# Cross attention on one core: a turn for every operation of the scheduler in place of a rank for each task

## The chip, the core and the metric

The kernel runs on one core of one Trainium2 chip. The metric is the time of one execution on the device in microseconds. A core has a matrix engine (TensorE, PE in the profile, with PEld for its weight loads), VectorE (DVE), ScalarE (ACT), GpSimd (POOL), and SyncE (SP), whose queue issues nearly all DMAs here. Each engine carries out its instructions in the order in which they stand in the program, and waits on semaphores for what the others deliver.

## The reference

`x` is (2, 2048, 640); `ctx_768` is (2, 128, 384), of which the first 124 rows are the text and the last 4 the adapter's tokens. There are 8 heads, in float32 throughout.

```python
query = hidden_states @ Wq
keyt, valt = enc @ Wk, enc @ Wv
hs = _mha(query, keyt, valt)                       # text: 2048 queries, 124 keys
ca_q1 = jnp.einsum('btc,th->bch', ca, Wq_ca)       # 384 rows, one per channel
indices = np.linspace(0, 384 - 1, unet_size).astype(np.int64)
ca_q1 = ca_q1[:, indices, :]
ca_hs1 = _mha(ca_q1, residual, residual)           # 384 different queries, 2048 keys
ca_hs2 = _mha(ca_hs1 @ Wq, ca @ Wk_ca, ca @ Wv_ca) # 4 keys
out = (hs + ca_hs2) @ Wout + b_out + residual
```

## The kernel before

**What is computed where.** The tokens of the two batches are cut into 8 blocks of 512 and 16 units of 256 (two tiles of 128 tokens each). For a block, x is loaded and transposed on VectorE (`xt`), multiplied with the adapter's folded weights (`yz_block`, tile `pyz`) and with Wq (`queries` for the first two blocks, `queries_fast` for the others, tile `pq`; the fast form computes a 2x2 split of the product with seven multiplications and sums of x and of Wq, and VectorE adds the parts up). For a unit, `text_scores` makes the scores of two tiles (`sc`), `softmax` their exponentials (`p`), which go to HBM and come back turned (`kept`, then `pT` by four loads); `hidden` multiplies them with the values (`ph`, copied to `hs`), and `text_out_fast` multiplies with Wout in four chains of products (`po`), each added by VectorE onto the rows of x. For a batch, `adapter` makes the scores of the 384 different queries twice: once for their maxima over 24 pieces (tile `s`, 4 PSUM banks, read by VectorE into `mx`), and once for their exponentials over 24 pieces (`s`, read by ScalarE into `ea`), which `contract` multiplies with the values (`acc`); `second` does the attention over four tokens and writes 384 rows (`o2`) to HBM. At the end GpSimd gathers a row of `o2` for each token onto a finished tile by an indirect DMA (`add_second`, line 2129), and SyncE stores the tile. Unit 15 has its gather ahead of its products, and is stored by half rows.

**Shapes of matmul.** A float32 matmul stands in the trace as two. Most products use four 128x32 tiles of the array side by side (`by_columns`, line 222: `pq`, `po`; line 210: `ph`, `acc`); `sc` uses two of 64x128, `s` four of 32x128, `pyz` eight of 64x32; transposes and the setup use the full 128x128.

**The order of the work.** It is fixed while the program is built. Each part above is a task: a Python generator that yields operations (`Do`) and starts further tasks (`Fork`). `Desk` replays the kernel with estimated durations: in `run` it takes, for each engine, the operations whose inputs and buffers are known, finds the earliest time at which one can start, and among those ready at that time picks the one with the lowest `order`, plus for TensorE a price for changing the tile shape (`change`). The engine with the earliest start issues. The instructions of an engine are kept in just that order. `order` is the rank of the task, or of the operation, plus an offset for the task out of the table `RANKS`, set by its name and number. An operation that may run on more than one engine stands in the queues of all of them, and the first to take it has it. Buffers are `Room`s of so many slots (`banks` for PSUM, `rows` for the tiles of x that become output, `hss` for `hs`); a slot is free from the time at which its last user is estimated to end. Durations come from `matmul`, `by_columns`, `transpose`, `__getattr__` (the other engines), `dma`, and `_mode` for a change of shape. A transfer's time is a queue of one channel: so long to issue, so long on the channel, and 2.8 us until it has landed.

In `stored`, a tile of a unit whose batch's `o2` isn't known yet when it is finished would be written to HBM and read back later (`early_`); otherwise it waits for its gather.

Of the kernel before, what the change touches and what calls it, by code (L numbers as in the profile page):

```python
# [8 lines left out]
F32 = mybir.dt.float32  # L9
# [50 lines left out]
class Task:  # L60
    def __init__(self, gen, rank, key, more):
        self.gen, self.rank, self.key, self.more, self.last = gen, rank, key, more, Event()


class Desk:
# [4 lines left out]
    WHOLE, SWITCH, LEAVE, ANOTHER = (P, P), 328.5, 9.9, 185.7  # L70
# [6 lines left out]
    MORE = {  # L77
        "v_transpose": 0.025, "v_stream_shuffle": 0.09, "v_scalar_tensor_tensor": 0.07, "v_reciprocal": 0.035,
        "a_activation": 0.045,
    }  # L80
    COLD = 5.2
    TAIL = {"PE": 0.25, "DVE": 0.18, "ACT": 0.2, "POOL": 0.25, "SP": 0.1, "NONE": 0.0}


    RANKS = {
        "adapter": {0: 1, 1: 2},
        "chain": {2: 8, 4: -11, 5: 7, 6: -2, 8: -11, 11: -4, 14: 11, 15: 16, 19: -14, 24: -4, 25: 3, 30: 3.1,
            32: 4, 34: 10, 36: 2, 41: 0.5, 42: 1, 43: 0.5, 44: -10, 45: -10, 48: -8, 50: -5, 51: -5, 52: 7,
            54: 10, 55: 10, 56: 10, 68: -4, 76: -3, 81: 2, 86: 2, 87: 3},
        "contract": {0: 5, 1: 4.5, 2: 8, 3: 8},  # L90
        "halves_away": {1: -4, 2: -2, 4: 4, 6: 6},
        "keys": {0: -10},
        "probabilities": {3: -8, 5: -4, 8: 12, 9: -3, 10: -2, 12: 6, 13: 6, 15: 7},
        "queries_fast": {0: 5, 3: 4},
        "rest_back": {1: 11, 4: 5, 7: 8, 9: 9, 10: 5, 14: 2},
        "second": {0: 2.3},
        "softmax": {0: 5, 2: -7, 3: 6.2, 4: -4, 7: -11, 8: 2, 10: -5, 12: -20, 14: -3, 17: 9, 20: -2, 21: 7,
            22: 7, 25: -5, 29: 2, 30: 6},
        "sums_of_wq": {0: 5.7},
        "text_scores": {0: -8, 1: 3.4, 12: 9},  # L100
        "values_weights": {0: -18},
        "x_load": {1: 4.2, 4: 5},
        "y_rows": {2: 2, 3: 6, 4: 4},
        "y_weights": {0: 1},
        "yz_block": {2: 16, 5: 3.5, 6: 5},
    }

    def __init__(self, tc):
        self.tc, self.nc, self.now, self.spent, self.mode = tc, tc.nc, 0.0, 0.0, None
        self.free = {e: 0.0 for e in self.ENGINES}  # L110
        self.queue = {e: [] for e in self.ENGINES}
        self.events, self.landed, self.channel, self.log, self.begun = {}, 0.0, 0.0, [], {}

# [6 lines left out]
    def begin(self, gen, rank):  # L120
        name = gen.__name__
        n = self.begun[name] = self.begun.get(name, -1) + 1
        task = Task(gen, rank, (name, n), self.RANKS.get(name, {}).get(n, 0.0))
        task.last.t = self.now
        self.go_on(task, None)

    def go_on(self, task, value):
        while True:
# [7 lines left out]
        op.task, op.at = task, Event()  # L136
# [45 lines left out]
    def issue(self, t, engine, op):  # L182
        for e in op.engines:
            self.queue[e].remove(op)
        self.now, self.spent, self.landed, self.engine = t, 0.0, None, engine
# [23 lines left out]
    def matmul(self, out, lhsT, rhs, **kw):  # L209
        self.pin(self.nc.tensor.matmul(out, lhsT, rhs, **kw))  # L210
        n = 1
        for size in rhs.shape[1:]:
            n *= size
# [3 lines left out]
        self.spent += self.slow() * (1 if one else 2) * max(n / 1.2, 107) / 1e3 / at_once  # L217

    def by_columns(self, out, lhsT, rhs, **kw):
# [3 lines left out]
        n = 1  # L223
        for size in rhs.shape[1:]:
            n *= size
        self._mode(P, P)
        self.spent += 2 * max(n / 1.2, 107) / 1e3

    def transpose(self, out, in_, ident):
        self.pin(self.nc.tensor.transpose(out, in_, ident))  # L230
        self._mode(P, P)
        self.spent += self.slow() * 0.115
# [4 lines left out]
    def __getattr__(self, name):  # L237

        side, _, what = name.partition("_")
        engine = {"v": self.nc.vector, "a": self.nc.scalar, "g": self.nc.gpsimd}[side]  # L240
        base, each = {"v": (0.06, 1.04), "a": (0.13, 0.77), "g": (0.1, 2.1)}[side]
# [2152 lines left out]
```

## Time and profile before

| what | value |
|---|---|
| median of 3 runs | 582.21 us (582.02 to 582.29) |
| the profiled execution | 581.8 us, of which 580.1 us are its span |
| granted clock of TensorE | 1.000 |
| first matmul, last matmul's end | 1.13 us, 576.4 us |
| scores `s` from and to | 52.7 us to 459 us |
| gathers from and to | 342.7 us to 567.5 us |
| DMA | 112.71 MB, 194 GB/s over the span |

The span runs from the first to the last instruction that the profiler saw on the core; times of single instructions are given from its start. A row of a group reads: line, engine, operation, what is written and what is read, shapes and count, then busy time and the mean of one in ns, then the idle time of the engine ahead of them and what ended it. A row in order of time reads: start, length, engine, line, operation, tiles, shapes, count, and in brackets the idle time ahead of it and what ended it.

### The profile page before, as it was taken

The numbers are of one execution on the slowest core, as the hardware profiler recorded it, in microseconds if no ns is written. First come the engines' busy times: TensorE is split into PE (matmuls) and PEld (weight loads), VectorE is DVE, ScalarE is ACT, GpSimd is POOL, SyncE is SP. The second block draws the span as 40 slices with busy tenths as digits, with TensorE's granted clock in tenths as the row PEclk, the third lists the DMA queues.
The fourth block names the chain that finished last, engine by engine and source line by source line (L and its number), as shares of the span: only waits on it lengthen the run. The fifth ranks groups of instructions, "written<-read, shape, count | busy, mean of one in ns | idle before, by whom it ended". The sixth has DMA issues, their size and how long they took to land.

```text
span 580.1 us, 19105 instructions
## 1 busy us (share of the span) xinstructions
PE 570.3 (98%) x8115; PEld 308.4 (53%) x8115; DVE 391.7 (68%) x645; ACT 309.8 (53%) x869; POOL 141.6 (24%) x200
## 2 busy tenths in 40 slices
PE   9999999999999999999999999999999999999997
PEld 8885334555555545455455445454455545545453
DVE  2446799999999756356999999973455253444443
ACT  2413376686566898689847447277877613002020
POOL 9102112012206411120114326050140312403241
PEclk9999999999999999999999999999999999999999
DMA  8897866979766888234999969999549487799995
GB/s 245 196 263 131 199 94 187 179 201 172 182 184 137 217 157 221 82 113 149 219 284 247 230 152 236 270 227 275 142 105 266 112 211 155 181 263 247 250 249 139
DMA packets 153039, 112.71 MB, mean 194 GB/s; under 512 B 83701, under 2 KB 126581, under 8 KB 152954
## 3 DMA queue, kind: packets, MB, share of 16 engines
q1 hardware_dynamic: 147322, 100.80, 67.5%
q0 software_dynamic: 5632, 10.69, 11.3%
q8 instruction: 64, 1.05, 0.8%
q14 instruction: 21, 0.17, 0.1%
HBM read 71.23 MB, written 40.22 MB: 192 GB/s over the span
## 4 chain that ended last, share of the span: by engine, by line
PE 64%; DVE 16%; DMA 8%; ACT 6%; issue 4%; SPq 1%; DVEq 0%; ACTq 0%
PE po L222 25%; PE pq L222 9%; PE ph L210 6%; DVE mx L245 6%; PE acc L210 5%; PE s L210 4%; PE pq L210 4%; PE sc L210 3%; ACT ea L245 3%; DMA kept<-eb 3%; DMA pT<-kept 2%; ACT p L245 2%; DVE m L245 2%; DVE q L245 2%; DVE eb L245 2%
## 5 line engine op out<-in xcount | busy, mean ns | idle before, releaser
L245 DVE TENSOR_REDUCE mx<-s 128x4 f32<-128x2048 f32 x48 | 109.4, 2280 | 4.1 <-PE s L210 4.1
L245 ACT ACTIVATE ea<-s 128x2048 f32<-128x2048 f32 x48 | 91.0, 1897 | 24.2 <-PE s L210 23.9
L245 ACT ACTIVATE p<-sc,m 128x124 f32<-128x124 f32 x256 | 90.2, 383 | 10.2 <-DVE m L245 9.7
L222 PE MATMUL po<-wout_sums,hs 128*32 128x320 f32 x1024 | 77.3, 433 | 0.0
L222 PE MATMUL po<-wout_sb,hs 128*32 128x320 f32 x960 | 74.2, 433 | 0.7 <-DVE x_more L245 0.7
L222 PE MATMUL pq<-xt,wq_sb 128*32 128x256 f32 (+1 forms) x928 | 66.3, 418 | 0.5 <-DVE mt L245 0.5
L245 DVE TENSOR_TENSOR x_more<-x_more,po 128x320 f32<-128x320 f32 x72 | 34.3, 483 | 45.5 <-PE po L222 45.4
L2129 POOL DMA_INDIRECT x_more<-o,query x18 | 27.9, 1550 | 124.3 <-DVE x_more L245 92.5
L245 ACT ACTIVATION_READ_ACCUMULATOR p<-sc,m 128x1 f32 x256 | 57.8, 226 | 0.0
L245 ACT COPY hs<-ph 128x512 f32<-128x512 f32 (+1 forms) x34 | 18.5, 551 | 65.8 <-PE ph L210 65.2
L222 PEld LDWEIGHTS po<-wout_sums,hs 128*32 128x32 f32 x1024 | 32.9, 110 | 34.1 <-issue 1.8
L210 PE MATMUL acc<-ea,y_sb 128*32 128x384 f32 (+2 forms) x768 | 51.0, 385 | 0.0
L222 PEld LDWEIGHTS po<-wout_sb,hs 128*32 128x32 f32 x960 | 30.4, 110 | 33.1 <-issue 1.5
L245 DVE TENSOR_REDUCE m<-sc 128x4 f32<-128x496 f32 x64 | 40.0, 662 | 10.4 <-PE sc L210 10.4
L245 DVE TENSOR_TENSOR last_rows<-last_rows,po 128x320 f32<-128x320 f32 x56 | 26.7, 481 | 27.9 <-PE po L222 27.5
L210 PE MATMUL ph<-pT,vpad 128*32 128x256 f32 x768 | 45.3, 380 | 0.1
L245 POOL TENSOR_TENSOR p<-p,r 128x992 f32<-128x992 f32 x8 | 14.8, 1846 | 125.0 <-DVE r L245 125.0
L222 PEld LDWEIGHTS pq<-xt,wq_sb 128*32 128x32 f32 x928 | 27.8, 109 | 29.6 <-issue 13.5
L245 DVE STREAM_TRANSPOSE eb<-p 128x1024 f32<-128x1024 f32 x32 | 39.4, 1233 | 5.6 <-DMA kept<-eb 5.5
L210 PEld LDWEIGHTS sc<-kmain,q 64*128 64x128 f32 x512 | 32.1, 187 | 13.7 <-issue 5.5
L210 PE MATMUL sc<-kmain,q 64*128 64x124 f32 x512 | 38.4, 285 | 0.2 <-ACT p L245 0.2
L245 ACT CAST rests<-landing 128x512 fp32r<-128x512 f32 x30 | 18.7, 635 | 36.2 <-PE sc L210 28.0
(216 smaller groups left out, 847.6 us busy)
## 6 DMA issues: line engine op xcount, KB each, us to landing
kept<-eb SPq DMA_DIRECT2D x32, 512.0 KB, 3.8
pT<-kept SPq DMA_DIRECT2D x64, 256.0 KB, 8.2
landing<-away SPq DMA_DIRECT2D x60, 128.0 KB, 4.3
xi<-in_x_dram SPq DMA_DIRECT2D x56, 128.0 KB, 4.6
x_more<-in_x_dram SPq DMA_DIRECT2D x18, 320.0 KB, 6.8
out_dram<-x_more SPq DMA_DIRECT2D x16, 320.0 KB, 6.6
last_rows<-in_x_dram SPq DMA_DIRECT2D x14, 320.0 KB, 7.2
out_dram<-last_rows SPq DMA_DIRECT2D x14, 320.0 KB, 10.0
```

Source lines behind the costliest of these rows:

```text
L210: self.pin(self.nc.tensor.matmul(out, lhsT, rhs, **kw))
L222: self.pin(self.nc.tensor.matmul(out[j : j + 32], lhsT[:, j : j + 32], rhs, **kw))
L245: self.pin(getattr(engine, what)(*args, **kw))
L2129: desk.pin(nc.gpsimd.indirect_dma_start(out=t, out_offset=None, in_=o2_of[b], in_offset=bass.IndirectOffsetOnAxis(ap=query[:, st : st + 1] ...
```

## The change

The table `RANKS` is emptied, and a table `TURNS` gives each of the 2353 operations of the 572 tasks a number of its own, by the task's path (the number of its start within its parent) and the operation's place in it. The first numbers of a path are: 2 the idle work, 4 the first loads, 5 to 16 the setup, 17 to 54 the blocks, 55 the adapter with 55.1 for the second batch, 56 to 71 the units 0 to 15. Where a path has turns, the price for a change of shape is 0, and TensorE may take an operation that is ready up to `AHEAD` = 0.368 us after the first. The estimates of durations are replaced as well: entering and leaving a tile shape have a price each, a matmul some ns more, VectorE and GpSimd wait for each other in operations with two inputs, a transfer has its own time to issue and on the channel, and a queue holds eight transfers in flight. What was done by counters in the code (when a slot of x, of q or of `hs` is free, when a tile is finished) are operations of their own on no engine. A finished tile of a unit below 15 always waits for its gather; the way by HBM is gone. The matmuls are the same and as many.

```diff
@@ class Desk
-    START = {(P, P): 0.107, (64, P): 0.143, (P, 64): 0.107, (64, 32): 0.1, (P, 32): 0.03}
-    DRAIN = {
-        ((P, P), (32, P)): 0.136, ((P, P), (64, P)): 0.035, ((P, P), (P, 64)): 0.056, ((P, P), (P, 32)): 0.067,
-        ((32, P), (P, 32)): 0.049, ((P, 64), (P, P)): 0.07, ((P, P), (P, P)): 0.0,
-    }
-    DRAINS = {(64, P): 0.172, (32, P): 0.108, (P, 32): 0.115}
+    AHEAD, IDLE = 0.368, 0.0
+    ENTER = {(P, P): 0.104, (64, P): 0.143, (64, 32): 0.16, (P, 32): 0.024, (32, P): 0.006}
+    EXIT = {(P, P): 0.07, (P, 32): 0.114}
+    SLOTS = 8
...
+    TURNS = {
+        ".1": [94], ".2": [8, 10, 18, 12, 20, 15, 7, 22, 0, 23, 28, 24, 19, 31, 32, 86], ".3": [60], ".4": [1, 13,
...
+        ".64.3.8": [2323], ".64.3.9": [2327, 2322, 2346], ".64.3.10": [2320, 2317, 2352], ".64.3.11": [2294, 2332,
+        2299, 2287, 2305, 2318, 2314, 2310], ".64.3.12": [2301, 2300, 2306, 2312], ".64.3.13": [2316, 2324],
+        ".64.3.14": [2303, 2304], ".65.1": [2014, 2062], ".65.2": [1122, 1214], ".65.2.1": [1135, 1130, 1132, 1138,
...
+        ".69.3.8": [1828], ".69.3.9": [1791, 2201, 2232], ".69.3.10": [1830, 2127, 2148], ".69.3.11": [1738, 1744,
...
+        ".71.3.12": [2350, 2344], ".71.3.13": [2319, 2329, 2321, 2336, 2339, 2342, 2309, 2347], ".71.3.14": [2328,
+        2311, 2341, 2345], ".71.3.15": [2335, 2338], ".71.3.16": [2334, 2333], ".72": [257, 259, 201, 282, 304, 312,
...
+    RANKS = {}
@@ begin, go_on
+        self.parent.forks += 1
+        task.path = f"{self.parent.path}.{self.parent.forks}"
...
+        op.task, op.at, op.num = task, Event(), task.ops
+        task.ops += 1
@@ change, order, run
-        if mode is None or mode == self.mode:
+        if mode is None or mode == self.mode or self.mode is None or self.TURNS:
             return 0.0
-        return self.LEAVE if self.mode == self.WHOLE else self.SWITCH if mode == self.WHOLE else self.ANOTHER
+        return self.CHANGE.get(self.KINDS[self.mode] + self.KINDS[mode], 0.0)
 
     def order(self, op):
+        if op.task.path in self.TURNS:
+            return self.TURNS[op.task.path][op.num]
         return (op.order() if callable(op.order) else op.order) + op.task.more
...
-                    t = min(x[0] for x in found)
+                    first = min(x[0] for x in found)
+                    ahead = self.AHEAD if e == "PE" else 1e-9
                     t, op = min(
-                        (x for x in found if x[0] <= t + 1e-9),
-                        key=lambda x: self.order(x[1]) + self.change(x[1].mode),
+                        (x for x in found if x[0] <= first + ahead),
+                        key=lambda x: self.order(x[1]) + self.change(x[1].mode) + self.IDLE * (x[0] - first),
                     )
@@ issue
+        if self.pairs:
+            self.spent += max(0.0, self.port[self.SHARED[engine]] - t)
+            self.port[engine] = t + self.spent
@@ _mode
+        if mode != self.mode:
+            self.spent += self.EXIT.get(self.mode, 0.0)
         if mode != self.mode or self.idle:
-            self.spent += self.START.get(mode, 0.0)
-            self.spent += self.DRAIN.get((self.mode, mode), self.DRAINS.get(self.mode, 0.1))
+            self.spent += self.ENTER.get(mode, 0.05)
@@ dma
-    def dma(self, out, in_, us, issue=0.45, more=2.8):
+    def dma(self, out, in_, us, issue=0.5, more=2.7):
 
         self.pin(self.nc.sync.dma_start(out, in_))
-        self.spent += issue
+        self.transfer("SP", us, issue, more)
+
+    def transfer(self, side, us, issue, more=2.7):
+
+        flights = self.flights[side]
+        self.spent = max(self.spent, flights.pop(0) - self.now) + issue
         self.channel = max(self.channel, self.now + self.spent) + us
         self.landed = self.channel + more
+        flights.append(self.landed)
@@ probabilities
-                lambda: dma(pT[R * j : R * (j + 1)].rearrange("p i k h a -> p i (k h a)"), by_keys[j], 1.1),
+                lambda: dma(pT[R * j : R * (j + 1)].rearrange("p i k h a -> p i (k h a)"), by_keys[j], 1.2, 0.48),
@@ add_second
-        desk.spent += 1.9
-        desk.landed = desk.now + desk.spent + 6.5
+        desk.transfer("POOL", 1.5, 1.57)
@@ one of the operations in place of a counter
+    def free_x(b, sb):
+
+        yield Do("NONE", lambda: None, [("x", b, sb)])
+        yield Do(
+            "NONE", lambda: None, [("used", b, sb, "yz"), ("used", b, sb, "q")], frees=[(xslots, xt[b, sb][1])]
+        )
@@ stored
+        yield Do("NONE", lambda: None, both)
         b, st = tiles(m)[k]
         t, i, _ = xr_of[m][k]
         rows_out = out[b, st * P : (st + 1) * P, :]
-        own = []
-        if gather_last[m] and not desk.known(("o2", b)):
-            part = hbm.tile([P, H], F32, tag=f"early_{m}_{k}", name=f"early_{b}_{st}")
-            op = yield Do("SP", lambda: dma(part, t, 1.3), both, frees=[(rows, i)])
-            yield Do("NONE", lambda: None, [op.at, ("o2", b)])
...
-            op = yield Do("SP", load, needs=[(rows, 1), (ending, 1)], rank=-1)
-            t, i, own = op.value, op.slots[0][0], [(ending, op.slots[1][0])]
-            both = [op.at]
-        if gather_last[m]:
-            op = yield Do("POOL", lambda: add_second(t, b, st), [*both, ("o2", b), "query"])
-            both = [op.at]
-        yield Do("SP", lambda: dma(rows_out, t, 1.3), both, frees=[(rows, i)] + own)
+        op = yield Do("POOL", lambda: add_second(t, b, st), [*both, ("o2", b), "query"])
+        yield Do("SP", lambda: dma(rows_out, t, 1.3, 0.41), frees=[(rows, i)])
```

More of the change, by code (lines that the diff above doesn't have):

```diff
@@ L1255, in queries @@
             own = [(qslots, 1)] if n not in q_of else []
-            op = yield Do("PE", part, [*after, "wq4"], needs=[(banks, 1), *own], mode=(P, P))
+            op = yield Do("PE", part, [*after, "wq4"], needs=[(banks, 1), *own], mode=(P, 32))
             pq, s, q = op.value, op.slots[0][0], q_of[n][0]
@@ L1879, in product @@
                     return po
-                op = yield Do("PE", product, [here, ("w2", u)], needs=[(banks, 1)])
+                op = yield Do("PE", product, [here, ("w2", u)], needs=[(banks, 1)], mode=(P, 32))
                 op = yield Do(
@@ L2243, in chain @@
                 op = yield Do(
-                    "PE", product, after + at + ready, needs=[(banks, 1)] if k == 0 else [], mode=(P, P), rank=rank
+                    "PE", product, after + at + ready, needs=[(banks, 1)] if k == 0 else [], mode=(P, 32), rank=rank
                 )
@@ L2266, in chain @@
-                ends.setdefault((m, i), []).append(op.at)
-                if not tile_left[m, i]:
-                    yield Fork(stored(m, i, ends[m, i]), 1)
+        reads = {(i, u): [] for i in range(2) for u in range(2)}
+        for n, steps in enumerate(chains):
+            for _, _, (place,) in steps:
+                reads[place].append(("sum", m, *place, n))
+        yield Fork(one(Do(
+            "NONE", lambda: None, [("chain", m, n) for n in range(len(chains))], frees=[(hss, at_hs)]
+        )), 0)
```

238 lines of the change are left out of this document (104 added, 134 removed), and 182 rows, old and new, of the table TURNS.

## The prediction

> **What bounds the kernel now.** I read the page first: how busy each engine is, and the chain that ended last.
>
> ```profile
> span 580.1 us, 19105 instructions
> ...
> PE 570.3 (98%) x8115; PEld 308.4 (53%) x8115; DVE 391.7 (68%) x645; ACT 309.8 (53%) x869; POOL 141.6 (24%) x200
> ...
> PE 64%; DVE 16%; DMA 8%; ACT 6%; issue 4%; SPq 1%; DVEq 0%; ACTq 0%
> ```
>
> TensorE has 9.8 us of idle time in all, and is the largest part of the chain. Nothing in this change takes a matmul away, so only what lies between matmuls can move. Next I looked at the sums by stretch (length, then busy time of PE, PEld, DVE, ACT and POOL with their counts, PE's granted clock, DMA share, GB/s).
>
> ```profile
> 60.00:180.00 120.00, 119.47 (x1668) 58.67 (x1662) 116.12 (x151) 77.70 (x291) 19.61 (x17) 1.00 0.74 169
> 180.00:320.00 140.00, 136.47 (x2127) 73.89 (x2128) 100.47 (x144) 109.11 (x288) 35.34 (x37) 1.00 0.74 188
> 320.00:460.00 140.00, 139.09 (x2112) 70.55 (x2108) 95.06 (x134) 88.89 (x219) 36.06 (x36) 1.00 0.82 204
> 460.00:580.00 120.00, 116.38 (x1798) 59.39 (x1790) 51.65 (x116) 17.52 (x34) 31.44 (x21) 1.00 0.85 208
> ```
>
> The clock is full throughout, so it can neither help nor hurt. TensorE stays above 97% in every stretch. VectorE comes close only in the first of them (116 of 120). The 3.6 us missing in the last stretch are the tail behind the last matmul.
>
> A busy TensorE is not one at its pace, so the third view is its order of time (start, length), which gives the price of each change of tile shape and the first matmul; the one row below it, from the chain in order of time, is the pace.
>
> ```profile
> 1.13 2.93 PE L210 MATMUL unread<-zeros 128*128 128x128 f32 x12 [1.13 <-DVE zeros L245]
> ...
> 70.60 4.50 PE L222 MATMUL pq<-xt,wq_sb 128*32 128x512 f32 x40
> 75.03 1.95 PE L210 MATMUL pyz<-xt,wyz 64*32 64x512 f32 x32
> 76.90 0.50 PE L210 MATMUL s<-zop,cop 32*128 32x512 f32 x4
> 77.33 2.78 PE L222 MATMUL pq<-xt,wq_sb 128*32 128x512 f32 x24
> 80.05 1.16 PE L210 MATMUL sc<-kmain,q 64*128 64x124 f32 x16
> 80.96 0.64 PE L210 MATMUL sc<-krest,rests 64*128 64x124 f32 x8
> 81.53 1.92 PE L222 MATMUL pq<-xt,wq_sb 128*32 128x512 f32 x16
> ```
>
> ```profile
> 557.00 19.42 PE po L222 x288
> ```
>
> The last row is an unbroken run: 19.42 / 288 = 0.0674 us for 320 columns with four 128x32 tiles at once, so about 0.107 for 512 columns. At that pace the 40 matmuls at 70.60 need 4.29, yet the next shape starts 4.43 later; the 24 at 77.33 need 2.57 and take 2.72. Leaving the 128x32 shape costs 0.14. The 64x32 run (75.03 to 76.90, eight tiles at once, 32 x 0.0537 = 1.72) loses 0.15. The 64x128 run (80.05 to 81.53) takes 1.48 for 24, of which the first 16 need 0.91: 24 x 0.057 = 1.37, so 0.11 is lost. The 32x128 run (76.90 to 77.33) takes 0.43 for 4 x 0.107: nothing is lost. For full 128x128 tiles I take the 0.14 of the nearest row.
>
> How many such changes are there? The three odd shapes have these pieces:
>
> ```profile
> L245 DVE TENSOR_REDUCE mx<-s 128x4 f32<-128x2048 f32 x48 | 109.4, 2280 | 4.1 <-PE s L210 4.1
> L245 ACT ACTIVATE ea<-s 128x2048 f32<-128x2048 f32 x48 | 91.0, 1897 | 24.2 <-PE s L210 23.9
> L210 PE MATMUL sc<-kmain,q 64*128 64x124 f32 x512 | 38.4, 285 | 0.2 <-ACT p L245 0.2
> L210 PE MATMUL pyz<-xt,wyz 64*32 64x512 f32 x256 | 15.6, 595 | 0.0
> ```
>
> So 96 pieces of s, 512 / 16 = 32 of sc, 256 / 32 = 8 of pyz. Walking all 8115 matmuls from the first row above to the one at 575.66 below, I count 269 changes of shape: 112 times the engine leaves 128x32, 20 times 128x128, 32 times 64x128, 97 times 32x128 and 8 times 64x32. Together 132 x 0.14 + 32 x 0.11 + 8 x 0.15 = 23.2 us.
>
> At the pace above, scaled by columns and tiles at once, the 8115 matmuls stream for 537.6 us. The span is then 1.1 (before the first) + 537.6 + 23.2 + 14.5 (waits) + 3.7 (tail). Of the waits about 3.5 lie before 57 us, in the start; 11 lie behind it. Two of the larger ones:
>
> ```profile
> 275.31 0.51 PE L210 MATMUL s<-zop,cop 32*128 32x512 f32 x4 [0.46 <-ACT ea L245]
> ...
> 406.94 0.75 PE L222 MATMUL po<-wout_sb,hs 128*32 128x320 f32 x8 [0.53 <-DVE x_more L245]
> ```
>
> They are short, some tenths of a us, and many: s waits until ScalarE or VectorE has emptied the one set of four banks, and a chain waits until VectorE has added its last product. That is what another order can remove.
>
> **The change part by part.** *Fewer changes of shape.* I sorted TensorE's 550 operations by their new turns, none ahead of an operation that its own task yields earlier, and put their shapes beside them: 248 changes, of which 107 leave 128x32, 15 leave 128x128, 28 leave 64x128 and 8 leave 64x32 (by the bare turns 244, with 105, 15, 30 and 8). That is 122 x 0.14 + 28 x 0.11 + 8 x 0.15 = 21.4 us against 23.2: -1.8. The turns are not the order itself (an operation whose inputs are late is passed over), so I keep -0.5 to -3.
>
> The Trainium skill, "TensorEngine Tiling (Array Packing)", Key Properties under Tiling Modes, says that every change of tiling mode drains TensorE. By that rule all 269 and 248 would cost alike, at the 0.14 above 21 x 0.14 = -2.9. The trace agrees for three shapes and not for 32x128, which is left without a loss.
>
> *Waits.* The scheduler's ready times get other constants, and its ties are broken for each operation by itself. Nothing in the rows shows what waits the new order leaves. The bounds: all 11 us behind the start go, or none does, or new ones come that the trace doesn't show. The price of each 128x32 exit in the new table (0.114 out, 0.024 in) is the 0.14 that I read above, while the old one has 0.067 to 0.136 by pair; TensorE is laid out nearer to what it does. I take half, -5.4, nearest to the middle of the two bounds, since waits of 0.2 to 0.5 us at hand-overs between engines are of the size of the errors that a static order must live with. The start keeps its 3.5: the loads behind it go out in the order that one task yields, which the turns cannot change.
>
> *Wait for a better operation.* TensorE may now let up to 0.368 us pass for an operation with a lower turn. It is in the turns' order or not at all; I put 0 in the sum. Idle time recorded between the matmuls is 9.8 - 1.1 - 3.7 = 5.0 today; ten such waits at their full length would add 3.7, which the range holds.
>
> *The tail.* Today it runs like this (VectorE, SyncE and GpSimd among TensorE), and the row below is the landing of all gathers:
>
> ```profile
> 567.52 1.54 POOL L2129 DMA_INDIRECT last_rows<-o,query  x1 [0.61 <-DVE last_rows L245]
> ...
> 575.66 0.72 PE L222 MATMUL po<-wout_sb,wout_sums 128*32 128x320 f32 x8
> 575.89 0.39 SPq L265 DMA_DIRECT2D out_dram<-last_rows  x1
> 576.45 0.49 DVE L245 TENSOR_TENSOR x_more<-x_more,po 128x320 f32<-128x320 f32 x1 [1.13 <-PE po L222]
> 576.97 0.33 SPq L265 DMA_DIRECT2D out_dram<-x_more  x1
> ```
>
> ```profile
> DMA to landing us min/median/max: 4.8/6.0/10.8
> ```
>
> The last gather goes out 8.9 us before the last matmul ends (567.52 to 576.4) and its store leaves 8.4 later, just ahead of the last half row. In the new turns unit 8 is last but one: its products end with the operations of turns 2314 and 2316, and unit 15 still has some 12 column products behind them, 12 x 8 x 0.0674 = 6.5 us. Less the addition (0.5), the gather of unit 8's second tile leaves 6 us before the last matmul ends instead of 8.9, so its store leaves some 2.9 later against the end, 2.4 behind the last matmul, where the half row's goes out 0.6 behind it. The store's own landing is the same 3.1 (576.97 to 580.1) for both: the tail grows by about +1.8. With the fastest gather (4.8, 3.6 less than here) it doesn't grow; with the slowest (10.8) it grows by 4.2.
>
> *Row tiles.* The branch that wrote a finished tile to HBM and read it back is gone; now such a tile is kept until its gather. The rows of x were read 32 times for 32 tiles, and no other load of that kind is on the page, so the branch took no time:
>
> ```profile
> pT<-kept SPq DMA_DIRECT2D x64, 256.0 KB, 8.2
> ...
> x_more<-in_x_dram SPq DMA_DIRECT2D x18, 320.0 KB, 6.8
> out_dram<-x_more SPq DMA_DIRECT2D x16, 320.0 KB, 6.6
> last_rows<-in_x_dram SPq DMA_DIRECT2D x14, 320.0 KB, 7.2
> out_dram<-last_rows SPq DMA_DIRECT2D x14, 320.0 KB, 10.0
> ```
>
> Unit 13 holds two of eight such tiles, the first from turn 1791 to its gather at 2201; the six others cover this, and no other work of GpSimd stands between that gather and the ones around it. If they didn't, a unit would begin late by one row load, 7 us, hidden again as long as other products are ready. The bookkeeping (a freed slot as an operation of its own) issues nothing: 0.
>
> **The sum.** 580.1 - 1.8 - 5.4 + 1.8 = 574.7. The profiled execution took 581.8, 1.7 over its span, and the median of the runs is 582.2, 2.1 over it: 574.7 + 2.1 = 576.8 us.
>
> **Rivals.** *Most waits go.* Nothing in TensorE's row forces them: VectorE and ScalarE have slack in all stretches but one. With 9 of 11 us gone, fewer changes (-2.5) and a tail that a quick gather hides: 580.1 - 9 - 2.5 + 0.5 + 2.1 = 571.2. Against it: s alternates with its evacuation through one set of banks, 2.28 and 1.90 us each, and that leaves the same tight hand-overs.
>
> *The waits only move.* One order's waits for another's, and the tail eats the fewer changes: 582.2 - 1.8 + 1.8 = 582.2. For it: the waits are errors of tenths of a us that any fixed order has. Against it: one of them (275.31) sits where a longer piece ahead of s would have covered it.
>
> *Late transfers, slower.* The place is ph, the first product of each unit, which needs the four pT loads of the unit, at 8.2 us in the median. The new constants let four loads on an idle channel land 4 x 1.2 + 0.5 + 2.7 = 8.0 after the first is issued, so there is no margin but what the turns leave. Engines run in the order fixed at build, so all later matmuls wait for a late pT. From (1.8 + 5.4 - 1.8) / 16 = 0.34 us per unit this eats the gain; at 0.5 us it gives 576.8 + 8 = 584.8. SyncE's queue is in order too: a pT load that stands behind a store is held until that store's gather has landed. Against it: today no wait of TensorE for a load is among the rows above, with the DMA engines 0.74 to 0.85 busy.
>
> **Chances.** Forecast (574 to 580.5) 0.55; most waits go 0.19; the waits move 0.11; late transfers 0.15. A measurement of this kernel tells 0.2% (1.2 us) from no change. Faster takes the first two and the lower part of the third: 0.78; same the middle of the third, 0.06; slower its rest and the fourth, 0.16. The range 571 to 584 leaves out some 0.09 below, from the second case, and 0.09 above, from the fourth.
>
> **What would show it.** The count of changes of shape: near 248, and at most 255; each exit still 0.14. Waits behind 57 us: 4 to 7 us by the same walk over all matmuls. Idle time before the first matmul and up to 57 us unchanged within 1. The last gather some 6 us ahead of the last matmul's end and the tail between 4 and 8. It is wrong if ph shows idle time ended by a pT load, if TensorE's idle time grows beyond 9.8, or if the tail exceeds 8.

## The result, and the profile after

The changed kernel takes 586.02 us (median of 5 runs, 585.63 to 587.74) against 582.29 for the kernel before (5 runs): a ratio of 1.0062, 95% interval 1.0042 to 1.0082. It is 0.6% slower, a small loss but clear of the noise, where the prediction said 576.8 and faster. Its profiled execution took 585.71 us, with a span of 584.0.

The page of the changed kernel, the lines that answer those shown of before:

```profile
span 584.0 us, 19117 instructions
...
PE 569.0 (97%) x8115; PEld 307.7 (53%) x8115; DVE 392.3 (67%) x630; ACT 312.9 (54%) x879; POOL 153.6 (26%) x212
...
PE 82%; DVE 7%; ACT 5%; DMA 5%; issue 2%; SPq 0%; ACTq 0%; DVEq 0%
```

TensorE is idle for 15.0 us now (584.0 - 569.0), not 9.8. The sums by stretch, with the bounds of the prediction's fence (length, busy time of PE, PEld, DVE, ACT and POOL with their counts, PE's granted clock, DMA share, GB/s), say where:

```profile
60.00:180.00 120.00, 119.72 (x1666) 61.14 (x1669) 119.04 (x151) 77.46 (x291) 24.69 (x20) 1.00 0.75 173
180.00:320.00 140.00, 134.31 (x2109) 73.59 (x2111) 101.48 (x146) 110.81 (x302) 35.97 (x37) 0.99 0.64 177
320.00:460.00 140.00, 137.34 (x2072) 70.06 (x2065) 96.76 (x137) 76.59 (x212) 39.15 (x38) 1.00 0.86 217
460.00:580.00 120.00, 118.53 (x1830) 58.04 (x1822) 47.19 (x102) 30.99 (x38) 34.79 (x26) 1.00 0.80 197
```

The second stretch lost 2.2 us of work on TensorE (136.47 to 134.31), at a clock of 0.99, and the third 1.8 (139.09 to 137.34). Cut finer, the loss sits in two places. First the changed kernel, then the one before, in 200 to 260 and in 320 to 350 us:

```profile
200.00:260.00 60.00, 56.75 (x908) 30.75 (x907) 35.53 (x57) 51.51 (x126) 6.94 (x5) 0.97 0.48 150
320.00:350.00 30.00, 27.60 (x404) 14.57 (x397) 25.76 (x35) 18.73 (x77) 10.57 (x11) 1.00 1.07 259
```

```profile
200.00:260.00 60.00, 59.19 (x941) 30.36 (x939) 32.88 (x59) 49.19 (x98) 11.00 (x9) 1.00 0.58 151
320.00:350.00 30.00, 29.65 (x422) 13.67 (x414) 29.31 (x33) 12.66 (x49) 8.52 (x10) 1.00 0.85 187
```

In the first place the DMA engines are half idle (0.48) and the clock is down; in the second they are full (1.07, before 0.85).

*The first place*, in order of time (start, length, engine, line, operation; in brackets the idle time ahead of it and what ended that). These are rows from the changed kernel's timeline, 202 to 216 us:

```profile
202.15 1.91 PE L405 MATMUL acc<-ea,y_sb 128*32 128x128 f32 x32
...
202.39 1.30 SPq L456 DMA_DIRECT2D z<-zs  x1
...
207.82 2.62 POOL L436 TENSOR_TENSOR x_sums<-xt,x_sums 128x512 f32<-128x512 f32 x2
...
208.31 0.01 DVE L436 LOAD_MASK_SELECT zs<-yz  x1 [5.23 <-DMA z<-zs]
208.34 0.76 DVE L436 STREAM_SHUFFLE zs<-yz 128x512 f32<-128x512 f32 x1
...
209.20 2.29 DVE L436 TENSOR_TENSOR p<-p,r 128x992 f32<-128x992 f32 x1
211.41 0.68 DVE L436 COPY q<-pq 128x512 f32<-128x512 f32 x1
...
212.15 1.07 PE L414 MATMUL pq<-xt,wq_sb 128*32 128x256 f32 x16 [2.82 <-DVE q L436]
...
213.82 1.94 PE L405 MATMUL acc<-ea,y_sb 128*32 128x128 f32 x16
```

Read it from below. TensorE waits 2.82 us for q, a copy of VectorE. VectorE runs its operations in the order of the build, and ahead of that copy stands the shuffle into zs, of which there is one buffer (`Room(1)`). It waits 5.23 us for the store that empties it. That store left SyncE at 202.39; in the scheduler's replay, which puts a time to every operation, it leaves at 199.6 and has landed at 203.1. The queue was 2.8 us late by then, and the store landed near 208.3. Behind the shuffle, p<-p,r takes 2.29 us beside GpSimd's two sums, where it takes 1.19 alone (the run with the store first, below). The Trainium skill, "SBUF — State Buffer", section "SBUF: two separate sides", says that VectorE, in an operation with two inputs in SBUF, and GpSimd share one pair of ports, which one of them holds for a whole instruction while the other stands. The trace agrees: the 1.10 us lost is nearly what GpSimd's second sum had left at 209.20 (1.24). How much of TensorE's 2.82 us this collision makes was not tested by itself; the rows put it at 1.10 at most.

The idle time has a price behind it. The same place, one microsecond to a row:

```profile
211.00:212.00 1.00, 0.00 (x0) 0.00 (x0) 1.00 (x2) 0.00 (x0) 0.00 (x0) 1.00 0.00 0
...
213.00:214.00 1.00, 1.00 (x17) 0.63 (x16) 1.00 (x3) 0.16 (x1) 0.00 (x0) 0.63 0.00 0
214.00:215.00 1.00, 1.00 (x16) 0.41 (x11) 0.98 (x2) 1.00 (x7) 0.00 (x0) 0.50 0.58 194
215.00:216.00 1.00, 1.00 (x16) 0.23 (x16) 0.00 (x0) 1.00 (x7) 0.00 (x0) 0.50 1.00 294
216.00:217.00 1.00, 1.00 (x16) 0.20 (x8) 0.22 (x2) 1.00 (x6) 0.00 (x0) 0.67 1.04 312
```

From 213 to 217 the granted clock is 0.50 to 0.67, and 16 products of acc last 1.94, where 32 of them took 1.91 at 202.15. TensorE counts as busy there and does about half the work.

*The second place*, rows from 332 to 348 us:

```profile
332.33 4.17 SPq L456 DMA_DIRECT2D landing<-away  x4
...
346.09 0.62 ACT L436 CAST rests<-landing 128x512 fp32r<-128x512 f32 x1 [3.96 <-DMA landing<-away]
346.62 0.85 ACT L436 COPY hs<-ph 128x512 f32<-128x512 f32 x2
...
347.25 1.21 PE L405 MATMUL sc<-kmain,q 64*128 64x124 f32 x14 [2.22 <-ACT hs L436]
```

The same pattern on another engine. ScalarE waits 3.96 us for four loads issued up to 336.5, which land near 346, as all DMA engines are full; behind that cast stand two copies to hs, and TensorE waits for these. Of the 24 products of this sc only the last 8 read what the cast writes (rests); the first 16 wait for nothing but the copies behind it, which empty the bank of PSUM that they write.

The tail, which the prediction lengthened by 1.8, answers with these rows (GpSimd, TensorE, VectorE, SyncE):

```profile
571.67 1.55 POOL L2324 DMA_INDIRECT last_rows<-o,query  x1 [0.30 <-issue]
...
579.04 1.26 PE L414 MATMUL po<-wout_sb,hs 128*32 128x320 f32 x16
579.83 1.03 DVE L436 TENSOR_TENSOR x_more<-x_more,po 128x320 f32<-128x320 f32 x2 [1.13 <-PE po L414]
580.34 0.87 SPq L456 DMA_DIRECT2D out_dram<-x_more  x2
```

The last matmul ends at 580.3, and 584.0 - 580.3 = 3.7 us follow, as before. The last gather goes out 8.6 us ahead of that end.

### The profile page after: what moved, and what is told of

Same layout as the page of the kernel before. It is cut to its first block, busy times and chain, and to the rows that moved or that the text cites. A ratio compares the mean times of both kernels' runs of the same rounds, so it can differ in the third digit from the quotient of the medians.

```text
span 584.0 us, 19117 instructions
## 1 busy us (share of the span) xinstructions
PE 569.0 (97%) x8115; PEld 307.7 (53%) x8115; DVE 392.3 (67%) x630; ACT 312.9 (54%) x879; POOL 153.6 (26%) x212
## 3 DMA queue, kind: packets, MB, share of 16 engines
q8 instruction: 64, 1.05, 0.7%
## 4 chain that ended last, share of the span: by engine, by line
PE 82%; DVE 7%; ACT 5%; DMA 5%; issue 2%; SPq 0%; ACTq 0%; DVEq 0%
PE po L414 24%; PE pq L414 21%; PE acc L405 7%; PE s L405 6%; PE ph L405 6%; PE sc L405 6%; PE pq L405 4%; PE pyz L405 2%; ACT ea L436 2%; DVE mx L436 2%; DMA pT<-kept 2%; DMA landing<-away 2%; ACT p L436 1%; PE pk L405 1%; PE pv L405 1%
## 5 line engine op out<-in xcount | busy, mean ns | idle before, releaser
L414 PE MATMUL po<-wout_sb,hs 128*32 128x320 f32 x928 | 72.1, 434 | 0.0
L405 PE MATMUL ph<-pT,vpad 128*32 128x256 f32 x768 | 47.2, 380 | 0.0
L436 ACT COPY hs<-ph 128x512 f32<-128x512 f32 (+1 forms) x31 | 16.9, 554 | 53.1 <-PE ph L405 52.3
L414 PEld LDWEIGHTS po<-wout_sb,hs 128*32 128x32 f32 x928 | 28.9, 110 | 31.2 <-issue 2.1
L436 ACT ACTIVATE p<-p,r 128x124 f32<-128x124 f32 x112 | 33.9, 385 | 12.7 <-DVE r L436 12.7
```

The lines of the kernel that those rows point to most:

```text
L414: self.pin(self.nc.tensor.matmul(out[j : j + 32], lhsT[:, j : j + 32], rhs, **kw))
L436: self.pin(getattr(engine, what)(*args, **kw))
```

## The experiments

Two of my theories stand behind the expectations. The first: the two places are the whole loss, each a single operation that waits for a late transfer and holds an in-order engine. The second, which is wider: the new transfer estimates are exact in the mean and leave no margin, so this order suffers more from any late transfer. The rival to both: an order of this tightness has such hand-overs wherever it is cut.

Where a run has another order, each engine is held to a written list, which is the list that the scheduler chose for the changed kernel, and only the operations named in the diff move; in the last two rows of the table the scheduler chooses again. All measured numbers first; waits are TensorE's, from the walk over all matmuls that the prediction used (time between starts beyond stream and change of shape), in the profiled execution, in all, in 200 to 260 and in 320 to 380 us. The ratio is to the kernel before on the same chip. Products slowed by a lower clock count as waits in this walk too. The profiled execution is one of several and need not be a typical one: with the store of z first (579.52), part of unit 5 later (579.83) and all of unit 5 later (578.16) it was the fastest of all, so the waits of these three rows are probably too low for their medians.

| run | median us | ratio (95%) | waits, 200–260, 320–380 |
|---|---|---|---|
| before | 582.29 | | 13.9, 1.5, 0.7 |
| after | 586.02 | 1.0062 (1.0042–1.0082) | 18.9, 5.4, 3.3 |
| after, again | 587.12 | 1.0113 (1.0071–1.0155) | 19.1, 6.5, 1.8 |
| shuffle to zs later | 584.96 | 1.0044 (1.0021–1.0067) | 18.0, 1.9, 6.1 |
| store of z first | 584.61 | 1.0042 (1.0023–1.0061) | 12.7, 1.1, 1.4 |
| landing first | 589.04 | 1.0112 (1.0088–1.0137) | 22.0, 5.4, 5.7 |
| all three | 587.82 | 1.0085 (1.0061–1.0109) | 22.2, 1.1, 9.6 |
| light rows, after | 586.85 | 1.0074 (1.0057–1.0091) | 21.1, 5.5, 4.0 |
| light rows, before | 582.67 | 1.0002 (0.9993–1.0012) | 14.8, 2.6, 0.8 |
| more copies, after | 590.72 | 1.0145 (1.0108–1.0182) | 22.3, 5.5, 6.0 |
| more copies, before | 585.64 | 1.0062 (1.0035–1.0088) | 17.9, 1.5, 0.8 |
| light rows, zeroed singly | 582.81 | 1.0014 (1.0003–1.0025) | 15.4, 4.7, 1.2 |
| the same, store first | 578.73 | 0.9947 (0.9930–0.9963) | 12.1, 1.2, 0.1 |
| part of unit 5 later | 583.51 | 1.0019 (0.9996–1.0042) | 13.1, 1.2, 2.4 |
| all of unit 5 later | 581.21 | 0.9992 (0.9967–1.0017) | 11.4, 1.1, 1.1 |
| the same, hs first | 580.68 | 0.9974 (0.9962–0.9986) | 13.4, 1.1, 1.5 |
| ranks, new estimates | 607.30 | 1.0429 (1.0406–1.0453) | 38.6, 9.3, 7.8 |
| turns, old estimates | 616.23 | 1.0575 (1.0545–1.0604) | 48.7, 9.9, 7.4 |

**The first place.** One run moves the shuffle on VectorE, one the store on SyncE.

```diff
 VectorE
-zs<-yz (second half)   r   p<-p,r   q<-pq
+r   p<-p,r   q<-pq   zs<-yz (second half)
```

> The changed kernel's own order, instruction for instruction, with one operation moved: VectorE's second shuffle of block 6 (zs<-yz), which stood idle 5.2 us until the store of the first (z<-zs) had landed, comes behind the reciprocal, the multiplication of p and the copy of q that were queued behind it. Theory (engines that run in order stand behind transfers that land later than the order has room for): TensorE's wait of 2.8 us at 212 us and the slow matmuls behind it (about 1.1 us) go, so 4.0 us less than the changed kernel: 582.0, ratio to the kernel before 0.9995. Rival one (VectorE's work there is slow because GpSimd reads at the same time: p took 2.29 instead of 1.19): only 0 to 1 us less, 585 to 586. Rival two (the order loses by its dependences, and a wait removed comes back further on): TensorE's wait at 212 goes, but the time stays at 585 or more.

```diff
 SyncE
-away<-wq_sums   away<-x_sums   kept<-eb   y<-yt   z<-zs
+z<-zs   away<-wq_sums   away<-x_sums   kept<-eb   y<-yt
```

> The changed kernel's own order with one transfer moved in SyncE's queue: the store z<-zs of block 6, issued at 202.4 us, goes ahead of four stores that left between 199.7 and 202.4. Theory (late transfer): VectorE's wait of 5.2 us for it shrinks by 2.7, TensorE's of 2.8 us to 0.1, and the matmuls behind it stay at full pace: 3 to 4 us less than the changed kernel, 582 to 583. If the store is late by its travel and not by its place in the queue: less than 1 us, 585 or more. Rival one (VectorE slowed by GpSimd): below 1 us as well.

Rows of the run with the store first, the same operations as above:

```profile
200.23 0.43 SPq L660 DMA_DIRECT2D z<-zs  x1
...
203.43 0.01 DVE L640 LOAD_MASK_SELECT zs<-yz  x1 [0.31 <-DMA z<-zs]
...
205.55 1.19 DVE L640 TENSOR_TENSOR p<-p,r 128x992 f32<-128x992 f32 x1
206.66 0.68 DVE L640 COPY q<-pq 128x512 f32<-128x512 f32 x1
...
209.18 1.05 PE L618 MATMUL pq<-xt,wq_sb 128*32 128x256 f32 x16
```

The store leaves 2.2 us earlier, the shuffle waits 0.31 instead of 5.23, the collision with GpSimd is gone, and TensorE has no wait here. With either edit the waits of 200 to 260 us fall from 5.4 to below 2: the chain is as read. The time follows only in part: 584.96 and 584.61, where my theory had 582.0 and 582 to 583. The profiled execution with the store first took 579.52, but all but one of its 12 runs lie between that and 586.06. The other run gives a reason: there the second place grew from 3.3 to 6.1 us. It changes from execution to execution (the same kernel, run again, had 1.8 there, and 587.12 all the same).

**The second place, first try.** The landing loads go ahead of another unit's row load and a store:

```diff
 SyncE
-x rows (unit 2, second)   kept<-eb   landing<-away x4
+landing<-away x4   x rows (unit 2, second)   kept<-eb
```

> The changed kernel's own order with four transfers moved in SyncE's queue: the four loads landing<-away issued from 332 to 336 us go ahead of a load of x rows and a store of kept. ScalarE waited 3.96 us for them, with the copies of hs behind it that TensorE's scores waited for (2.2 us at 347 us). Theory (late transfers): the loads leave about 2.6 us earlier, TensorE's wait at 347 goes nearly: 2 us less than the changed kernel, 584.0. Rival (the DMA engines are full there, 0.97 busy, so that any order of the queue moves the wait to what is put back, the load of rows or the store): 0 to 0.5 us less, or more time.

The rival held: 589.04. The cast is in time, and the next in line is late. Rows of this run:

```profile
336.73 0.52 SPq L660 DMA_DIRECT2D kept<-eb  x1
...
347.02 1.25 DVE L640 STREAM_TRANSPOSE eb<-p 128x1024 f32<-128x1024 f32 x1 [4.19 <-DMA kept<-eb]
...
348.27 2.24 DVE L640 TENSOR_REDUCE mx<-s 128x4 f32<-128x2048 f32 x1
...
350.56 0.80 PE L609 MATMUL s<-zop,cop 32*128 32x512 f32 x4 [3.53 <-DVE mx L640]
```

Now it is VectorE's transposition into the one eb buffer, whose store took some 10 us; mx stands behind it, and s behind mx. Changing the order of one queue thus only named another victim in the same stretch. The last run of this set makes all three edits:

> All three moves together on the changed kernel's own order. Theory (a few waits behind late transfers make the loss): 4.0 + 2.0 = 6 us less than the changed kernel, 580.0, ratio to the kernel before 0.996, below 1. Rival (a wait removed comes back further on, the order is simply longer): 584 or more, ratio 1.003 or more.

The rival held again: 587.82. Its first place is clean (1.1 us), and in the second s waits 4.92 us for mx behind the same eb. These moves within a stretch of full DMA engines did not cure it.

**Less and more traffic.** To take the cause away instead of moving it, the 32 row loads of x become 1/20 of their size (so x is added in 32 of its 640 columns only); to make it worse, each gets a copy beside it. Both in both kernels:

```diff
-                dma(t, x[b, st * P : (st + 1) * P, :], 1.1, 0.4)
+                dma(t[:, :32], x[b, st * P : (st + 1) * P, :32], 1.1, 0.4)
```

```diff
                 dma(t, x[b, st * P : (st + 1) * P, :], 1.1, 0.4)
+                copy = hbm.tile([P, H], F32, tag=f"copy_{m}_{st}", name=f"copy_{m}_{st}")
+                desk.pin(nc.sync.dma_start(copy, x[b, st * P : (st + 1) * P, :]))
```

> The turns' order, instruction for instruction, but each of the 32 loads of a row tile of x takes 32 of its 640 columns (16 KB instead of 320 KB, so some 9.7 of the 112.7 MB less); the products are still added to whole tiles, zeroed once by GpSimd, so the text rows have x added in 32 columns only. My theory (exact transfer estimates, no margin: a stretch of 320 to 350 us in which the DMA engines are full holds VectorE's and ScalarE's in-order operations behind late transfers, and TensorE behind them): waits of TensorE in 320 to 380 us fall from 4.5 (2.3 of them one wait behind ScalarE's hs) to below 2, the wait at 212 us stays, since no row loads run there, and the time falls to 581 to 583.5. The rival (the waits are hand-overs between engines that this order has whatever the transfers do): 585 to 587, with the wait near 347 still above 2 us.

> The same cut of the row loads with the ranks' order. My theory (this order has slack for late transfers already): within 1 us of its own time, 581 to 583. If the lighter traffic speeds both kernels alike, by 3 us or more, the margin is not what tells them apart.

> The turns' order, with one more copy of 320 KB behind each of the 32 loads of a row tile (from x to a scratch in HBM that nobody reads; the scheduler doesn't count it). My theory: no margin, so the waits in 320 to 380 us and in the later stretches grow, 591 to 605 us, at least 5 above the 586 of the plain kernel. The rival (waits don't hang on transfers): 586 to 588.

> The same copies with the ranks' order. My theory: its slack takes most of them, 582 to 587, so the growth is at least 4 us less than that of the turns' order. If both grow by the same amount within 2 us, the turns' order is no more sensitive to transfers than the ranks'.

The light run missed its number for a reason of its own. Its rows near 322 us:

```profile
319.95 2.23 POOL L2255 MEMSET last_rows<- 128x2560 f32 x1
...
322.14 2.32 POOL L436 TENSOR_TENSOR hs<-hs 128x256 f32<-128x256 f32 x3
...
324.51 1.93 PE L414 MATMUL po<-wout_sb,hs 128*32 128x320 f32 x16 [2.03 <-POOL hs L436]
```

The zeroing that the cut makes necessary stood ahead of GpSimd's sums of hs and cost TensorE 2.03 us: the same kind of wait, made by my edit. The wait behind the cast was gone (4.0 - 2.2 for the wait at 324.5 leaves 1.8 us in the stretch, much of it slow products at a granted clock of 0.50 from 325 to 328), yet a time with both in it decides nothing, so I made this run again (below).

The heavy runs went against my wider theory, which had 591 to 605 for the turns' order and a growth at least 4 us larger than that of the ranks' order. Measured against before, the copies add 0.0062 (0.0035 to 0.0088) to the ranks' order, and 1.0145 against 1.0062 and 1.0113 for the plain kernel, so 0.003 to 0.008, to the turns' order. By the medians both grow by the same within 2 us, so nothing shows that the turns' order is more sensitive to traffic in general; the intervals leave room for a difference of some 4 us either way. The longest wait of its heavy run, 3.25 us at 332.43, follows 3.55 us of VectorE on the store of eb: the pattern of the run with landing first. In the plain kernel it has two bad places.

**Are they all of it?** The zeroing goes row tile by row tile, with and without the store first:

```diff
+                if at[0] not in cleared:
+                    cleared.append(at[0])
+                    desk.pin(nc.gpsimd.memset(t, 0.0))
                 dma(t[:, :32], x[b, st * P : (st + 1) * P, :32], 1.1, 0.4)
```

> Again the turns' order with row loads of x of 32 columns, but GpSimd zeroes each row tile by itself ahead of its first load (0.6 us each instead of twice 2.2 us at once; in the first form one of those stood ahead of two sums of hs). x is added in 32 columns only. My theory (full DMA engines hold the landing loads at 332 us, ScalarE's cast waits for them, hs for the cast, sc for hs): no wait above 1 us in 320 to 350 us, waits of 320 to 380 us below 2, the wait of 3 us at 212 unchanged, time 582.5 to 584.5. The rival (the waits in 320 to 350 are the order's own): one wait above 2 us there again, and 585 to 587.

> The same with the store of z taken ahead of three other issues in SyncE's queue, as in the run with the store first; x is added in 32 columns only. If the two places are all that makes the turns' order slower than the ranks': both waits gone, total waits 12 to 14 us, time 578 to 580.5, faster than before. If there is a third cause (something that the two waits only cover), it stays at 583 or above.

By the times as the first theory had it: 582.81, with 3.0 us left at 212 and nothing above 1 us in 324 to 380 (GpSimd's zeroing still costs TensorE 1.0 at 322.6, which I had not expected), then 578.73 within 578.40 to 579.06. The latter's sums for the two places:

```profile
200.00:260.00 60.00, 59.42 (x975) 33.43 (x975) 38.66 (x65) 55.28 (x134) 8.20 (x7) 1.00 0.53 162
320.00:350.00 30.00, 30.00 (x448) 15.90 (x444) 27.78 (x36) 18.14 (x73) 10.48 (x11) 1.00 1.05 239
```

With both gone the turns' order beats the ranks' by 0.5%, and by the traffic cut alone the ranks' order gained nothing (1.0002). No third cause of size shows. Yet the DMA engines are as full in 320 to 350 as before (1.05 against 1.07): a full stretch alone does not make the wait. What did change is how soon the four landing loads got through: SyncE issued them in 2.77 us instead of 4.17, and the cast has no wait for them.

**With all the work.** Unit 5's transfers land some 16 us ahead of their first use in the replay; they move behind unit 1's (the expectations call these units 13 and 9 by mistake). First the last two of its pT loads and both rows, then all four pT loads, then ScalarE's cast behind the copies to hs as well:

```diff
 SyncE (and the store of z first)
-landing x4   pT 5 x4, rows 5   kept   out   pT 1 x4   landing x2   out   landing   kept   landing
+landing x4   kept   out   pT 1 x4   pT 5 x4   landing x2   out   landing   kept   rows 5   landing
 ScalarE (last run only)
-rests<-landing   hs<-ph   hs<-ph
+hs<-ph   hs<-ph   rests<-landing
```

> All work done; the store of z first, and in SyncE's queue two of unit 13's four pT loads behind unit 9's four, and its two row loads of x behind the next store of kept (they are needed some 17 us after the place they had). My theory: with 1.2 MB less in 330 to 345 us, landing and kept come in time, and the wait at 341 to 350 stays below 1 us in nearly every run: 579.5 to 582, with a spread below that of the store alone (579.5 to 588.3). If the full stretch only moves to 350 to 365 us: a wait of 2 us or more there, and 584 to 586.

> The same with all four pT loads of unit 13 behind unit 9's: 1.7 MB less in 330 to 345 us. My theory: as the last or a little better, 579 to 582. If the moved loads come late, ph of unit 13 waits for pT near 365 us, and the time is 584 or more.

> All work done; the store of z first, all pT and row loads of unit 13 later (as the run late_61_all), and in ScalarE's queue the two copies to hs ahead of the cast of the landing load. My theory (what is left of the second place is that cast): sc no longer hangs on the landing load, nearly all runs at 578 to 580.5, median 578.5 to 580.5, faster than before. If the slow ones of late_61_all (582 to 584.6) come from another place: the same spread, median 580.5 to 582.5.

The first stays at 583.51 (579.83 to 585.70), between the ranges that I gave for the two theories. The second is at 581.21, some runs at 578.2 to 579.9 and some at 582.5 to 584.6. The third narrows the spread, 580.13 to 582.31 in 12 runs, but its median of 580.68 misses the 578.5 to 580.5 of my theory and lies in the range that I gave for another place. It is faster than before by 0.26% (0.14 to 0.38). Its rows at the second place:

```profile
339.95 0.59 ACT L640 COPY hs<-ph 128x512 f32<-128x512 f32 x1 [1.07 <-PE ph L609]
340.76 0.37 ACT L640 COPY hs<-ph 128x256 f32<-128x256 f32 x1 [0.22 <-PE ph L609]
341.54 0.62 ACT L640 CAST rests<-landing 128x512 fp32r<-128x512 f32 x1 [0.41 <-DMA landing<-away]
341.70 1.16 PE L609 MATMUL sc<-kmain,q 64*128 64x124 f32 x16
```

The cast still waits for its load, 0.41, but sc no longer waits for the cast: its first 16 products run beside it, and the 8 that read rests come after. The granted clock says the same. With all of unit 5 later, the five executions above 582.4 us have 0.994 to 0.997, the five below 580 have 0.999 to 1.000; with hs first as well, 11 of 12 have 0.999 or more. So the executions with a halved clock are nearly gone with that edit, which speaks for the cast as their cause; no trace of one of them was taken, and the two runs were on different chips. The DMA engines stay full here too (1.01 in 320 to 350). With all the work done this order has the lowest median of both kernels, and is 2 us behind the one with light rows.

**Turns and transfer estimates apart.** The new transfer estimates without the turns, the turns with the old transfer estimates, and the whole again; the estimates for the engines stay as they are in each kernel. One pair of lines out of many, from the first:

```diff
-                    "SP", lambda u=u: dma(away[:, u], zs, 1.0), frees=[(zss, i)],
+                    "SP", lambda u=u: dma(away[:, u], zs, 0.3, 0.47), frees=[(zss, i)],
```

> The kernel before (a task's ranks) with the new transfer estimates alone, which gives another order out of the same ranks. If the estimates themselves are what costs (no slack for a late transfer): slower than before by 3 us or more, 585 to 600. If the loss belongs to the turns' order alone: 580 to 584.

> The changed kernel with the old transfer estimates: the same turns, other ready times, so operations pass over each other where the annealing didn't have them. If turns are good only under the replay that they were annealed in: 590 to 615. If the old estimates give back slack and nothing else: 578 to 584.

> The changed kernel as it is, on this chip beside the others: 585 to 588, the waits at 212 (about 3 us) and 347 (2 to 3.5 us) again. If it comes out at 583 or below here, the comparisons with it across chips tell nothing.

Both are far worse, and both lie above the ranges that I gave: 607.30 and 616.23, with 38.6 and 48.7 us of waits. The first number alone would fit "the estimates cost"; the second speaks against it, since the old estimates cost the turns even more. Either order was found under its own replay, and got worse under the other one; what the turns or the estimates contribute can't be read from these two runs. The whole again came out at 587.12, as expected, with the wait at 212 (2.82 us) and only 0.6 us at 347.

## Why the prediction was wrong

The sum, term by term, against the profiled span (580.1 to 584.0, +3.9):

- *Changes of shape*, predicted -1.8: the walk counts 261, not 248; 124 exits at 0.14, 32 at 0.11, 8 at 0.15 make 22.1 instead of 23.2, so -1.1. The price of an exit was right for the three shapes that the rows gave (0.138, 0.106 and 0.16 by the same walk); the 0.14 taken over for full tiles comes to about 0.09. The count was too low; the prediction named a reason, that operations whose inputs are late are passed over, and no run tests it.
- *Waits behind 57 us*, predicted -5.4: they went from 10.7 to 16.3, so +5.6. This step failed. The prediction put it "TensorE is laid out nearer to what it does. I take half, -5.4". A replay nearer to TensorE's pace says nothing of a store that leaves SyncE 2.8 us late. In its place stand two waits of other engines that pass on to TensorE: 5.4 - 1.5 = 3.9 us more in 200 to 260 and 3.3 - 0.7 = 2.6 more in 320 to 380, less 0.9 elsewhere. The prediction had also put the clock aside ("it can neither help nor hurt"); about 1.1 us of the loss are products at half the clock behind the wait at 212. Even without them the size was too large. With both places relieved, 8.6 us are left behind 57 us in the fastest execution (all of unit 5 later), so -2.1 and not -5.4; with hs first as well some 10.7 are left, as many as before, so nothing, and the gain of that order is about that of the changes of shape and the start. Of the waits left, 1.08, 0.96 and 0.64 us near 275, 294 and 490 come back in nearly all orders made from these turns. The replay has the first of them too (1.25 us), so the turns were chosen with it; it does not have the two others.
- *Tail*, predicted +1.8: 0.0. The last gather went out 8.6 us ahead of the end, not 6.
- *The start and the rest*, predicted 0: -0.5 and 0. Row tiles caused no extra load (32 in both), and no wait for one is among those above. What TensorE's look-ahead does was not tested by itself.

Together -1.1 + 5.6 + 0.0 - 0.5 = +4.0, against +3.9.

Of the rivals, "late transfers, slower" came true in kind and not in place: I put it at ph and its pT loads, where no wait of this kind appears in the changed kernel. That its price was near (584.8 against 586.0) is luck: it was 0.5 us for each of 16 units, and two waits made the loss. I looked only at transfers on which TensorE waits itself. The two that cost are awaited by VectorE and ScalarE, with operations behind them that TensorE needs at once: the shuffle into zs is not for the product that waited, and the cast only for a third of it. The chance of 0.15 for it was too low for that reason. "Waits only move" has its part: one order's hand-overs did go for another's, with 0 to 2.1 us to the good.

## What to carry to other kernels

In an order fixed at build, list for each transfer not who needs its data but what stands behind the waiting operation on its engine: an operation with a single buffer (zs, eb) or a late load ahead of a copy that TensorE needs is where a late transfer costs. The DMA share by stretch shows where transfers can come late. Where it was full here, moving one transfer ahead of another only chose the next victim; what brought the time down with all the work done was to move transfers with time to spare and to take the copies that TensorE needs ahead of the operation that waits, while the stretch stayed full. And a table of turns and the estimates under which it was found belong together.

## What the runs showed of the hardware

A wait of TensorE can cost more than itself. In the changed kernel the granted clock fell to 0.50 right behind the wait of 2.82 us, for some 3 us; in the same kernel run again it was 0.50 from 212 to 218 us, and 16 products of 1.07 us took 1.94. The length of the wait did not decide it alone. With light rows zeroed singly, as profiled, the same wait had no such row behind it, and its products took their 1.07:

```profile
212.56 1.07 PE L618 MATMUL pq<-xt,wq_sb 128*32 128x256 f32 x16 [2.82 <-DVE q L640]
...
214.00 1.07 PE L609 MATMUL acc<-ea,y_sb 128*32 128x128 f32 x16
```

In the first light run the shorter wait of 2.03 us, at 324.51, did have one:

```profile
326.00:328.00 2.00, 2.00 (x20) 0.85 (x16) 0.44 (x1) 1.58 (x6) 0.00 (x0) 0.50 1.04 330
```

The wait of 2.22 us at 347.25 had none. The Trainium skill, "TensorE: Matmul & The Clock Gate", section "What's actually happening", says that the clock is halved after an idle window of about 3.4 us. The trace agrees with the half, but it came after idle times shorter than that.

The granted clock of an execution tells whether it was halved on the way, and not whether there was a wait: 1.000 for before as profiled, 0.997 and 0.994 for the changed kernel, 0.993 and 0.994 for landing first and all three, 0.999 where both places are relieved, but 0.999 as well for the light run above that kept its wait of 2.82 us. Seven of the ten executions of that kernel have 0.997, so whether the clock is halved differs from one execution to the next. The order with the fewest such waits also repeated better: 578.40 to 579.06 in 4 runs with both gone, 585.83 to 592.47 in 4 of the changed kernel run again.
